# Attention scores of four heads: one kind to a stretch instead of half and half

## The chip, the core and the metric

The kernel runs on one core of a Trainium2 chip. The core has five engines, each with its own in-order queue: TensorE (PE, matmuls, with its weight loads shown apart as PEld), VectorE (DVE), ScalarE (ACT), GpSimd (POOL) and SyncE (SP, which issues the DMAs here). Matmuls write to PSUM, eight banks of 512 fp32 columns on 128 partitions; DVE and ACT read it. The metric is device time in microseconds of one execution, and a kernel's time is the median of its runs.

## The reference

For each of 16 sequences of 512 tokens with 512 channels, one transformer block: layer norm, attention of 32 heads of 16 channels, layer norm of its result and a residual sum; then layer norm, a gated feed-forward part of 1408 channels, layer norm, residual sum. The part the change touches is this:

```
q, k = rope(split_heads(x @ Wq.T + bq)), rope(split_heads(x @ Wk.T + bk))
scores = einsum('bhqd,bhkd->bhqk', q, k) / sqrt(dh)
scores = where(causal, scores, -inf)
weights = softmax(scores, axis=-1)
out = einsum('bhqk,bhkd->bhqd', weights, v)
```

The remaining lines are dense products: v, q, k and the output projection in fp32, gate, up and down products with split operands (a rounded part and the remainder) of type fp32r.

## The kernel before

**Groups and steps.** Four heads make a group, eight groups a batch (sequence), so there are 128 groups; group n is worked in five steps, `one_step(work, n, i)` for i = 0 to 4. A step emits, in this order: what earlier steps put off to it (`later`), in step 0 the loads of q and k of group n + 2 (`load_group`), one stretch of score matmuls (`scores`) with the ACT and DVE work on them, in step 2 the turning of the maxima (`turn_maxima`), a piece of dense work (`next(work)`), and in steps 3 and 0 the products of weights and values (`values`). All engines keep the order of the program: `InOrder` pins every instruction, so an instruction that waits holds back all that stand behind it on its engine.

**Two kinds of scores.** The softmax needs each row's maximum before the exponential. So the scores are computed twice. First as queries by keys (`S_PARTS`): DVE adds a mask of -1e30 on the diagonal blocks of 128 x 128 and takes the maximum along the keys, negated, into `nm`. `turn_maxima` transposes the 16 columns of maxima on PE (`pm`), ACT rounds them (`nmh`), DVE takes the remainder (`nml`), and a step later two DMAs place both as rows in `mx`. Then as keys by queries (`ST_PARTS`), with a third matmul that adds the negated maxima (`one` times `mx`): ACT takes the exponential of these straight into the weights `pa` and `pc`, POOL zeroes the part above the diagonal of diagonal blocks (`affine_select`), and `values` multiplies them with v. k is held as two fp32r pieces, `kh` and `kl`, so a part of the first kind takes two matmuls for each head, a part of the second kind three. The four heads sit in four strips of 32 rows, and their four matmuls run side by side; I call them a set.

**The banks.** Each head has one bank; `sc` is two tiles of two banks. In every step each bank holds both kinds, 256 columns each: the left half for weights, the right half for maxima (`at_s`). ACT and DVE work crosswise, ACT on the heads 0 and 1 while DVE has the heads 2 and 3, and then the other way round (lines 622 to 627). The next stretch begins when both are done, since its first set writes all four banks. A group's work on scores is 30 sets, ten exponentials of 512 elements, eight masks of 256, ten maxima of 512, and one small minimum that joins two partial maxima.

**The dense work.** `run_list` cuts the batch's list of dense products into pieces, one to a step, in proportion to `SHARES` (line 43), which gives a weight to each of the five steps; a unit of cost is four or two matmul passes of 512 columns, 0.27 for an fp32r matmul. It avoids a cut shortly after the end of a product. The products go through three PSUM buffers (`psum`, tag `d`), which a product's tail on ACT and DVE frees. Items such as `rest` and `store` of `qk_block` are laid behind a product at a given distance (`merge`). The tail and rest of a q or k block form a loop over ACT, DVE and POOL on single buffers `ya` and `ys`: ACT copies (`ys`), DVE multiplies with the cosine (`ya`), POOL multiplies with the sine, DVE adds, ACT rounds (`yh`), POOL subtracts (`yl`).

**Opening and end.** Before group 0 the maxima of groups 0 and 1 have to be made, in the steps from (-2, 2) on. The first list (v, q and k of the second batch) is spread over 46 of the 48 steps from there to the end of the first batch. The last batch has no q, k and v of a next one to make.

Of the kernel before, what the change touches and what calls it, by code (L numbers as in the profile page):

```python
# [24 lines left out]
NB = T // P  # L25
NC = C // P
NG = H // 4
WIDTH = H * W + 32 - W + 1
STEPS = 5
MM = 1.0  # L30
TR = 0.15
M1 = 0.27

HALF = T // 2
ST_PARTS = [[(0, 0, 256, 0)], [(0, 256, 256, 0)], [(1, 128, 256, 0)], [(1, 384, 128, 0), (3, 384, 128, 128)], [(2, 256, 256, 0)]]
S_PARTS = [[(3, 0, 256, 0)], [(3, 256, 256, 0)], [(0, 0, 128, 0), (2, 0, 128, 128)], [(2, 128, 256, 0)], [(1, 0, 256, 0)]]
S_DIAG = [None, 128, 0, 128, 128]  # L40
ST_DIAG = [0, None, 0, 128, 0]

SHARES = [2.3, 3.8, 3.8, 2.4, 3.5]


class InOrder:
# [14 lines left out]
class Block:  # L61
# [54 lines left out]
    def constants(self):  # L116
        nc, a, con = self.nc, self.a, self.const
# [23 lines left out]
        for name in ("bo", "dscale"):  # L141
# [3 lines left out]
        self.gh = con.tile([P, self.NF], FP, tag="gh", name="gh")  # L145
        self.gu = con.tile([P, self.NF], FP, tag="gu", name="gu")

        m = self.mask = con.tile([P, P], mybir.dt.bfloat16, tag="mask", name="mask")
        nc.gpsimd.memset(m, 0.0)
        nc.gpsimd.affine_select(  # L150
            out=m, in_=m, compare_op=ALU.is_ge, fill=-BIG, base=0, pattern=[[-1, P]], channel_multiplier=1
        )
        self.sc = [self.ps_sc.tile([P, 2, T], FP, tag=f"sc{k}", name="sc") for k in range(2)]
        self.v17 = []
        for i in range(2):
            t = con.tile([P, NB, WIDTH], FP, tag=f"v17_{i}", name=f"v17_{i}")
# [432 lines left out]
            ks.append(t)  # L589
        self.qs[n], self.ks[n] = q, ks  # L590

    def scores(self, n, m, i):

        todo = []
        st = 0 <= n < self.B * NG
        part = (i + 3) % STEPS
        at_s = HALF if n >= 0 or i % 2 else 0
        for j in range(4):
            r, r2 = slice(32 * j, 32 * j + 32), slice(32 * j, 32 * j + 2)
            todo.append([])  # L600
            if 0 <= m < self.B * NG:
                q, ks = self.qs[m], self.ks[m]
                for qb, k0, w, at in S_PARTS[part]:
                    at += at_s
                    out, x = self.sc[j // 2][:, j % 2, at : at + w], q[r, ts(qb, P)]
                    todo[-1] += [(out, x, ks[0][r, k0 : k0 + w], True, False), (out, x, ks[1][r, k0 : k0 + w], False, True)]
            if st:
                q, ks, mx = self.qs[n], self.ks[n], self.mxs[n]
                for kb, q0, w, at in ST_PARTS[i]:
                    out, x = self.sc[j // 2][:, j % 2, at : at + w], q[r, q0 : q0 + w]  # L610
                    todo[-1] += [
                        (out, ks[0][r, ts(kb, P)], x, True, False),
                        (out, ks[1][r, ts(kb, P)], x, False, False),
                        (out, self.one[r2, :], mx[r2, q0 : q0 + w], False, True),
                    ]

        for k in range(len(todo[0])):
            for t in todo:
                out, l, r, first, last = t[k]
                self.pe.matmul(out, l, r, start=first, stop=last)  # L620

        for two in (slice(0, 2), slice(2, 4)):
            other = slice(2 - two.start, 4 - two.start)
            if st:
                self.weights(n, i, two)
            if 0 <= m < self.B * NG:
                self.maxima(m, part, self.sc[other.start // 2][:, :, at_s : at_s + HALF], other)

    def maxima(self, m, part, s, two):
        if m not in self.nms:  # L630

            self.nms[m] = self.tile([P, 2, 4, NB], "nm", bufs=2)
        full = self.nms[m]
        nm = full[:, :, two]
        at = S_DIAG[part]
        if at is not None:
            d = s[:, :, at : at + P]
            self.dve.tensor_tensor(d, d, self.mask.unsqueeze(1).to_broadcast(list(d.shape)), ALU.add)
        out = [nm[:, 0, :, 3], nm[:, 1, :, 1], nm[:, :, :, 0].rearrange("p x j -> p j x"), nm[:, 0, :, 2], nm[:, 0, :, 1]][part]
        if part == 2:  # L640
            s = s.rearrange("p j (x t) -> p j x t", x=2)
        self.dve.tensor_reduce(out=out, in_=s, axis=AX.X, op=ALU.max, negate=True)
        if part == 4 and two.start == 0:
            self.dve.tensor_tensor(full[:, 0, :, 2:4], full[:, 0, :, 2:4], full[:, 1, :, 0:2], ALU.min)

    def turn_maxima(self, m):
        p = self.psum("pm")
        self.pe.transpose(p[0:16, 0:P], self.nms.pop(m)[:, 0].rearrange("p j b -> p (j b)"), self.ident)
# [11 lines left out]
    def weights(self, n, i, two):  # L660
        if i % 2 == 0 and two.start == 0:
            self.pts[n, i // 2] = self.tile([P, 4, HALF], "pc", bufs=1) if i == 4 else self.tile([P, 4, T], "pa", bufs=2)
        at = HALF * (i % 2)
        pt = self.pts[n, i // 2][:, :, at : at + HALF]
        self.act.activation(pt[:, two], self.sc[two.start // 2][:, :, 0:HALF], AF.Exp, scale=0.25)
        at = ST_DIAG[i]
        if at is not None and two.start:
            d = pt[:, :, at : at + P]
            self.pool.affine_select(
                out=d, in_=d, compare_op=ALU.is_ge, fill=0.0, base=0, pattern=[[0, 4], [1, P]], channel_multiplier=-1  # L670
            )

    def values(self, n, lot):
        b, g = divmod(n, NG)
        if lot == 0:
            self.avs[n] = self.ps_av.tile([P, T], FP, tag="av", name="av")
        av = self.avs[n]
        for kb, w, k, at in ([(0, 512, 0, 0)], [(1, 384, 1, 0), (3, 128, 1, 384), (2, 256, 2, 0)])[lot]:
            for j in range(4):
                h = 4 * g + j  # L680
                self.pe.matmul(
                    av[32 * j : 32 * j + 32, T - w : T],
                    self.v17[b % 2][:, kb, h * W : h * W + 32],
                    self.pts[n, k][:, j, at : at + w],
                    start=(kb == 0),
                    stop=(kb == 2),
                )
        if lot:
            for k in range(3):
                del self.pts[n, k]  # L690
# [27 lines left out]
    def run_list(self, L, steps, first=0):  # L718
# [109 lines left out]
    def one_step(self, work, n, i):  # L828
        for f, args in self.todo.pop(self.step, []):
            f(*args)  # L830
        if i == 0 and n + 2 < self.B * NG:
            self.load_group(n + 2)
        self.scores(n, n + 2 if i >= 2 else n + 1, i)
        if i == 2 and 0 <= n + 1 < self.B * NG:
            self.turn_maxima(n + 1)
        next(work, None)
        if i == 3 and 0 <= n < self.B * NG:
            self.values(n, 0)
        if i == 0 and 0 <= n - 1 < self.B * NG:
            self.values(n - 1, 1)  # L840
        self.step += 1

    def front(self):
# [152 lines left out]

    def batches(self):
        B = self.B
        work = self.run_list(self.first_list(), 46, 2)
        self.load_group(0)  # L1000
        for n, i0 in ((-2, 2), (-1, 0)):
            for i in range(i0, STEPS):
                self.one_step(work, n, i)
        for b in range(B):
            if b:
# [8 lines left out]
                work = self.run_list(L, NG * STEPS)  # L1014
# [4 lines left out]
        work = self.run_list(L + self.downs(B - 2, None, (0, 1), True, True), STEPS + 2)  # L1019
# [65 lines left out]
```

## Time and profile before

| what | value |
|---|---|
| median of 3 runs | 3304.48 us (3301.31 to 3305.98) |
| profiled execution | 3305.37 us |
| its span | 3303.5 us |
| mean granted PE clock | 0.974 of full speed |
| PE busy | 3036.6 us |
| DVE busy | 2168.4 us |
| ACT busy | 1602.6 us |
| POOL busy | 1326.7 us |
| DMA | 143 GB/s on the mean |

The profile is one execution. A line of the groups gives the engine, the operation, output and inputs by tile names, the shapes (partitions x elements) and the count; behind the first bar the busy time of the group and the mean of one in ns; behind the second the idle time of the engine just before them and what ended it. A line of the waits gives who waited for whom, the total, how often, and the longest. In the timeline the first number is the start, the second the duration, in us. Matmuls are pipelined, so their durations overlap: their cost is read from start to start.

### The profile page before, as it was taken

Reading aid. Unit: us, or ns where it says so; the run is one execution under the profiler, and the core shown is the slowest. Engines: PE = TensorE matmul, PEld = TensorE weight load, DVE = VectorE, ACT = ScalarE, POOL = GpSimd, SP = SyncE. Lnnn points to the kernel's source line nnn. Section 1 sums busy time; section 2 is a strip of 40 time slices with the busy share of each in tenths; the row PEclk is TensorE's granted clock in tenths of the full one; section 3 lists DMA queues with packets and bytes.
Section 4 is the critical chain, followed back from the end, with each engine's and each line's share of the span. In section 5 each row is a group of like instructions: output and inputs, shape, how many; then the busy total and the mean of one; then the engine's idle time right before and its main releaser. Section 6 shows DMA issues by size and latency. Waiting matters only on the chain. (4 is left out here: it accounts for less than half of the span.)

```text
span 3303.5 us, 69520 instructions
## 1 busy us (share of the span) xinstructions
PE 3036.6 (92%) x26378; PEld 1813.2 (55%) x26378; DVE 2168.4 (66%) x4253; ACT 1602.6 (49%) x2758; POOL 1326.7 (40%) x1677
## 2 busy tenths in 40 slices
PE   6778999999999999999999999999999999989898
PEld 3334564646556465554646556465564646546556
DVE  5565767766676676767767676676767766677743
ACT  5344545445544545545444554545445454554432
POOL 4133445343444424344342444424344442443443
PEclk9888999999999999999999999999999999999999
DMA  7444534535343453534445343453534445343322
GB/s 255 157 136 140 176 108 147 164 127 186 103 156 128 149 171 123 171 110 145 150 135 179 104 158 130 147 164 124 171 111 150 144 145 169 112 144 130 127 97 76
DMA packets 271973, 472.07 MB, mean 143 GB/s; under 512 B 45920, under 2 KB 50016, under 8 KB 271200
## 3 DMA queue, kind: packets, MB, share of 16 engines
q1 hardware_dynamic: 271200, 466.49, 43.4%
q8 instruction: 212, 3.47, 0.4%
q10 hardware_dynamic: 432, 1.05, 0.1%
q14 instruction: 129, 1.06, 0.1%
HBM read 345.79 MB, written 125.30 MB: 143 GB/s over the span
## 5 line engine op out<-in xcount | busy, mean ns | idle before, releaser
L56 ACT ACTIVATE pa<-sc 128x512 f32<-128x512 f32 x1024 | 607.0, 598 | 783.6 <-PE sc L56 409.0
L56 DVE TENSOR_REDUCE nm<-sc 128x2 f32<-128x512 f32 (+1 forms) x1280 | 877.0, 692 | 122.2 <-PE sc L56 86.5
L56 DVE TENSOR_TENSOR sc<-sc,mask 128x256 f32<-128x256 f32 x1024 | 437.2, 427 | 469.0 <-PE sc L56 396.8
L56 POOL TENSOR_SCALAR_AFFINE_SELECT pa<-pa 128x512 f32<-128x512 f32 x384 | 244.0, 636 | 969.7 <-ACT pa L56 631.9
L56 PEld LDWEIGHTS sc<-kh,q 32*128 32x128 f32 x3072 | 156.9, 186 | 492.9 <-issue 172.8
L56 PE MATMUL sc<-kh,q 32*128 32x256 f32 (+1 forms) x3072 | 276.9, 357 | 111.6 <-DVE nm L56 79.4
L56 PE MATMUL pd<-wd,hl 128*128 128x512 f32 x704 | 283.9, 403 | 24.7 <-POOL hl L56 24.7
L56 ACT ACTIVATE pc<-sc 128x512 f32<-128x512 f32 x256 | 151.4, 597 | 302.2 <-PE sc L56 175.3
L56 PE MATMUL pg<-xntf,wf 128*128 128x512 f32 x704 | 286.0, 406 | 9.7 <-DVE ya L56 6.4
L56 PE MATMUL pd<-wd,hh 128*128 128x512 f32 x704 | 289.0, 411 | 2.8 <-ACT hh L56 2.8
L56 POOL TENSOR_TENSOR hl<-ht,hh 128x512 fp32r<-128x512 f32 (+1 forms) x192 | 229.0, 1193 | 145.6 <-ACT hh L56 144.0
L56 PE MATMUL pg<-xntfl,wf 128*128 128x512 f32 x704 | 286.3, 407 | 0.2 <-DVE xntfl L56 0.2
L56 PE MATMUL av<-pa,v 128*32 128x512 f32 (+2 forms) x3072 | 282.4, 471 | 0.0
L56 PE MATMUL pu<-xntfl,wf 128*128 128x512 f32 x704 | 281.1, 399 | 0.0
L56 PE MATMUL pu<-xntf,wf 128*128 128x512 f32 x704 | 279.3, 397 | 0.0
L56 PE MATMUL pk<-xnta,w 128*128 128x512 f32 x480 | 259.4, 667 | 4.1 <-DVE ya L56 4.1
L56 POOL TENSOR_TENSOR yl<-ya,yh 128x512 fp32r<-128x512 f32 x128 | 162.9, 1273 | 201.9 <-ACT yh L56 201.9
L56 PE MATMUL pq<-xnta,w 128*128 128x512 f32 x480 | 236.9, 625 | 5.0 <-ACT xntf L56 4.3
L56 PE MATMUL po<-w,oc 128*128 128x512 f32 x512 | 238.4, 602 | 2.5 <-DMA w<-in_wo 2.0
L56 POOL TENSOR_TENSOR ln_rstd<-ln_ve,neghalf 128x1 f32<-128x1 f32 x256 | 146.8, 573 | 229.9 <-DVE ln_ve L56 229.7
L56 PE MATMUL sc<-q,kh 32*128 32x256 f32 (+1 forms) x3072 | 227.1, 279 | 0.1
L56 PE MATMUL sc<-mx,one 2*128 2x256 f32 (+1 forms) x3072 | 226.4, 277 | 0.1
(123 smaller groups left out, 5374.6 us busy)
## 6 DMA issues: line engine op xcount, KB each, us to landing
wf<-wgs SPq DMA_DIRECT2D x352, 256.0 KB
q<-qd SPq DMA_DIRECT2D x128, 256.0 KB
kh<-kd SPq DMA_DIRECT2D x128, 256.0 KB
kl<-kd SPq DMA_DIRECT2D x128, 256.0 KB
od<-ot SPq DMA_DIRECT2D x128, 256.0 KB
w<-in_wo SPq DMA_DIRECT2D x68, 256.0 KB
xr<-in_x SPq DMA_DIRECT2D x66, 256.0 KB
w<-in_wq SPq DMA_DIRECT2D x64, 256.0 KB
```

The costliest lines, as they stand in the source:

```text
L56: return self.tc.keep_in_program_order(f(*args, **kwargs))
```

## The change

A stretch now holds scores of one kind in steps 0 to 3, of up to 512 columns a head: in step 0 keys 0 to 127 by all 512 queries for weights; in step 1 the query blocks 2 (384 keys) and 0 (128 keys) for maxima; in step 2 the key blocks 3 (128 queries) and 1 (384 queries) for weights; in step 3 the query block 3 (512 keys) for maxima. Step 4 holds both, 256 columns each: key block 2 for weights, query block 1 for maxima. The maxima of step 1 are those of group n + 1, those of steps 3 and 4 of group n + 2 (`AHEAD`). `sc` is one tile of four banks. An exponential takes the four heads at once, 2048 elements in steps 0 and 2 and 1024 in step 4; so do mask and maximum. The mask tile is doubled to 256 columns for step 1, which has two diagonal blocks a head. POOL zeroes two blocks in one instruction in step 2. No maximum is in two parts any more, so the small minimum is gone. A group's work on scores is 20 sets, three exponentials, three masks, four maxima. The values follow in three bursts, at the end of steps 1, 3 and 0, instead of two. SHARES has new weights; the opening starts at step (-2, 3), and its list is spread over all of the 47 steps.

```diff
-ST_PARTS = [[(0, 0, 256, 0)], [(0, 256, 256, 0)], [(1, 128, 256, 0)], [(1, 384, 128, 0), (3, 384, 128, 128)], [(2, 256, 256, 0)]]
-S_PARTS = [[(3, 0, 256, 0)], [(3, 256, 256, 0)], [(0, 0, 128, 0), (2, 0, 128, 128)], [(2, 128, 256, 0)], [(1, 0, 256, 0)]]
-S_DIAG = [None, 128, 0, 128, 128]
-ST_DIAG = [0, None, 0, 128, 0]
-
-SHARES = [2.3, 3.8, 3.8, 2.4, 3.5]
+ST_SETS = [[(0, 0, 512, 0)], [], [(3, 384, 128, 0), (1, 128, 384, 128)], [], [(2, 256, 256, 0)]]
+S_SETS = [[], [(2, 384, 0), (0, 128, 384)], [], [(3, 512, 0)], [(1, 256, 256)]]
+AHEAD = [0, 1, 0, 2, 2]
+
+SHARES = [2.3, 3.1, 3.0, 2.8, 3.9]
...
-        self.sc = [self.ps_sc.tile([P, 2, T], FP, tag=f"sc{k}", name="sc") for k in range(2)]
+        self.sc = self.ps_sc.tile([P, 4, T], FP, tag="sc", name="sc")
...
-        for two in (slice(0, 2), slice(2, 4)):
-            other = slice(2 - two.start, 4 - two.start)
-            if st:
-                self.weights(n, i, two)
-            if 0 <= m < self.B * NG:
-                self.maxima(m, part, self.sc[other.start // 2][:, :, at_s : at_s + HALF], other)
+        if there(n) and ST_SETS[i]:
+            self.weights(n, i)
+        if there(m) and S_SETS[i]:
+            self.maxima(m, i)
+
+    def maxima(self, m, i):
+        if m not in self.nms:
+            self.nms[m] = self.tile([P, 4, NB], "nm", bufs=2)
+        w = P * len(S_SETS[i])
+        d = self.sc[:, :, T - w :]
+        self.dve.tensor_tensor(d, d, self.mask[:, 0:w].unsqueeze(1).to_broadcast(list(d.shape)), ALU.add)
+        for qb, w, at in S_SETS[i]:
+            self.dve.tensor_reduce(
+                out=self.nms[m][:, :, qb], in_=self.sc[:, :, at : at + w], axis=AX.X, op=ALU.max, negate=True
+            )
...
+    def weights(self, n, i):
+        w = HALF if i == 4 else T
+        pt = self.pts[n, i // 2] = self.tile([P, 4, w], "pc" if i == 4 else "pa", bufs=1 if i == 4 else 2)
+        self.act.activation(pt, self.sc[:, :, 0:w], AF.Exp, scale=0.25)
+        if i == 2:
+            d = pt[:, :, 0:HALF]
+            pat = [[0, 4], [0, 2], [1, P]]
+        else:
+            d, pat = pt[:, :, 0:P], [[0, 4], [1, P]]
+        self.pool.affine_select(out=d, in_=d, compare_op=ALU.is_ge, fill=0.0, base=0, pattern=pat, channel_multiplier=-1)
...
-        self.scores(n, n + 2 if i >= 2 else n + 1, i)
+        self.scores(n, i)
...
+        if i == 1 and 0 <= n < self.B * NG:
+            self.values(n, 0)
         if i == 3 and 0 <= n < self.B * NG:
-            self.values(n, 0)
+            self.values(n, 1)
         if i == 0 and 0 <= n - 1 < self.B * NG:
-            self.values(n - 1, 1)
+            self.values(n - 1, 2)
...
-        work = self.run_list(self.first_list(), 46, 2)
+        work = self.run_list(self.first_list(), 47, 3)
         self.load_group(0)
-        for n, i0 in ((-2, 2), (-1, 0)):
+        for n, i0 in ((-2, 3), (-1, 0)):
```

More of the change, by code (lines that the diff above doesn't have):

```diff
@@ L146, in constants @@
         self.gu = con.tile([P, self.NF], FP, tag="gu", name="gu")
-        m = self.mask = con.tile([P, P], mybir.dt.bfloat16, tag="mask", name="mask")
+        m = self.mask = con.tile([P, 2 * P], mybir.dt.bfloat16, tag="mask", name="mask")
         nc.gpsimd.memset(m, 0.0)
-        nc.gpsimd.affine_select(
-            out=m, in_=m, compare_op=ALU.is_ge, fill=-BIG, base=0, pattern=[[-1, P]], channel_multiplier=1
-        )
-        self.sc = [self.ps_sc.tile([P, 2, T], FP, tag=f"sc{k}", name="sc") for k in range(2)]
+        for i in range(2):
+            x = m[:, ts(i, P)]
+            nc.gpsimd.affine_select(
+                out=x, in_=x, compare_op=ALU.is_ge, fill=-BIG, base=0, pattern=[[-1, P]], channel_multiplier=1
+            )
+        self.sc = self.ps_sc.tile([P, 4, T], FP, tag="sc", name="sc")
         self.v17 = []
@@ L590, in load_group, with scores @@
         self.qs[n], self.ks[n] = q, ks
[L592 to L597, printed above, removed]
+    def scores(self, n, i):
+        m = n + AHEAD[i]
+        there = lambda g: 0 <= g < self.B * NG
+        todo = [[] for _ in range(4)]
         for j in range(4):
             r, r2 = slice(32 * j, 32 * j + 32), slice(32 * j, 32 * j + 2)
-            todo.append([])
-            if 0 <= m < self.B * NG:
[L602 to L606, printed above, removed]
-            if st:
[L608 to L611, printed above, removed]
+            if there(m):
+                for qb, w, at in S_SETS[i]:
+                    q, ks = self.qs[m], self.ks[m]
+                    out, x = self.sc[:, j, at : at + w], q[r, ts(qb, P)]
+                    todo[j] += [(out, x, ks[0][r, 0:w], True, False), (out, x, ks[1][r, 0:w], False, True)]
+            if there(n):
+                for kb, q0, w, at in ST_SETS[i]:
+                    q, ks, mx = self.qs[n], self.ks[n], self.mxs[n]
+                    out, x = self.sc[:, j, at : at + w], q[r, q0 : q0 + w]
+                    todo[j] += [
                         (out, ks[0][r, ts(kb, P)], x, True, False),
@@ L620, in scores @@
                 self.pe.matmul(out, l, r, start=first, stop=last)
-        for two in (slice(0, 2), slice(2, 4)):
-            other = slice(2 - two.start, 4 - two.start)
-            if st:
-                self.weights(n, i, two)
-            if 0 <= m < self.B * NG:
-                self.maxima(m, part, self.sc[other.start // 2][:, :, at_s : at_s + HALF], other)
-    def maxima(self, m, part, s, two):
-        if m not in self.nms:
[L632 to L644, printed above, removed]
+        if there(n) and ST_SETS[i]:
[3 more added lines that the diff above has]
+    def maxima(self, m, i):
+        if m not in self.nms:
+            self.nms[m] = self.tile([P, 4, NB], "nm", bufs=2)
+        w = P * len(S_SETS[i])
+        d = self.sc[:, :, T - w :]
+        self.dve.tensor_tensor(d, d, self.mask[:, 0:w].unsqueeze(1).to_broadcast(list(d.shape)), ALU.add)
+        for qb, w, at in S_SETS[i]:
+            self.dve.tensor_reduce(
+                out=self.nms[m][:, :, qb], in_=self.sc[:, :, at : at + w], axis=AX.X, op=ALU.max, negate=True
+            )
     def turn_maxima(self, m):
         p = self.psum("pm")
-        self.pe.transpose(p[0:16, 0:P], self.nms.pop(m)[:, 0].rearrange("p j b -> p (j b)"), self.ident)
+        self.pe.transpose(p[0:16, 0:P], self.nms.pop(m).rearrange("p j b -> p (j b)"), self.ident)
         hi, lo = [self.tile([16, P], i, bufs=1, dtype=FR) for i in ("nmh", "nml")]
@@ L658, in turn_maxima @@
         self.later(1, put)
[L660 to L671, printed above, removed]
+    def weights(self, n, i):
[8 more added lines that the diff above has]
+        self.pool.affine_select(out=d, in_=d, compare_op=ALU.is_ge, fill=0.0, base=0, pattern=pat, channel_multiplier=-1)
     def values(self, n, lot):
@@ L677, in values @@
         av = self.avs[n]
-        for kb, w, k, at in ([(0, 512, 0, 0)], [(1, 384, 1, 0), (3, 128, 1, 384), (2, 256, 2, 0)])[lot]:
+        pt = self.pts.pop((n, lot))
+        for kb, q0, w, at in ST_SETS[2 * lot]:
             for j in range(4):
@@ L683, in values @@
                     self.v17[b % 2][:, kb, h * W : h * W + 32],
-                    self.pts[n, k][:, j, at : at + w],
+                    pt[:, j, at : at + w],
                     start=(kb == 0),
@@ L687, in values @@
                 )
-        if lot:
-            for k in range(3):
-                del self.pts[n, k]
+        if lot == 2:
             del self.ks[n], self.qs[n], self.mxs[n]
```

## The prediction

> **What bounds the kernel now.** Read first the page's busy times, to see which engine leaves no room:
>
> ```profile
> PE 3036.6 (92%) x26378; PEld 1813.2 (55%) x26378; DVE 2168.4 (66%) x4253; ACT 1602.6 (49%) x2758; POOL 1326.7 (40%) x1677
> ```
>
> TensorE (PE) has work 92% of the span; VectorE (DVE) and ScalarE (ACT) do not fill theirs. So time comes from matmul time and from what makes PE wait. Next the groups by shape, for the price of each operation on scores:
>
> ```profile
> L56 DVE TENSOR_REDUCE nm<-sc 128x2 f32<-128x512 f32 x1024 | 699.6, 692 | 113.4 <-PE sc L56 86.5 <-ACT pa L56 0.3
> L56 ACT ACTIVATE pa<-sc 128x512 f32<-128x512 f32 x1024 | 607.0, 598 | 783.6 <-PE sc L56 409.0 <-DVE nm L56 347.0 <-PE pu L56 7.6
> L56 DVE TENSOR_TENSOR sc<-sc,mask 128x256 f32<-128x256 f32 x1024 | 437.2, 427 | 469.0 <-PE sc L56 396.8 <-ACT pa L56 56.1 <-ACT pc L56 11.1
> L56 PE MATMUL sc<-kh,q 32*128 32x256 f32 x2048 | 202.6, 383 | 69.5 <-DVE nm L56 37.3 <-ACT pa L56 7.8 <-ACT hh L56 7.0
> L56 PE MATMUL sc<-kh,q 32*128 32x128 f32 x1024 | 74.4, 305 | 42.2 <-DVE nm L56 42.1
> ```
>
> See that PE's waits ahead of a stretch of scores end with DVE's maxima. Then the waits, for what delays DVE itself:
>
> ```profile
> DVE ya L56 <- POOL yl L56: 122.9, 57, 2.2
> PE sc L56 <- DVE nm L56: 79.4, 82, 5.7
> PE pm L56 <- DVE ya L56: 37.0, 13, 3.0
> ```
>
> DVE stands still on `ya` (rotation of q and k) with the maxima queued behind it. Last the timeline of one step (a step 3 among gate and up products):
>
> ```profile
> 1597.85 0.39 PE L56 MATMUL sc<-kh,q 32*128 32x256 f32 x4
> ...
> 1598.70 0.28 PE L56 MATMUL sc<-mx,one 2*128 2x128 f32 x4
> 1598.91 0.50 PE L56 MATMUL pg<-xntfl,wf 128*128 128x512 f32 x1
> 1599.01 0.60 ACT L56 ACTIVATE pa<-sc 128x512 f32<-128x512 f32 x1 [2.82 <-PE sc L56]
> 1599.06 0.43 DVE L56 TENSOR_TENSOR sc<-sc,mask 128x256 f32<-128x256 f32 x1 [1.29 <-PE sc L56]
> ...
> 1600.31 0.60 ACT L56 ACTIVATE pa<-sc 128x512 f32<-128x512 f32 x1 [0.70 <-DVE nm L56]
> ...
> 1600.59 0.69 DVE L56 TENSOR_REDUCE nm<-sc 128x2 f32<-128x512 f32 x1
> ...
> 1600.95 1.07 PE L56 MATMUL av<-pa,v 128*32 128x512 f32 x8
> ...
> 1601.94 0.34 PE L56 MATMUL sc<-kh,q 32*128 32x128 f32 x4
> ```
>
> After the last set of four score matmuls (1598.70) ACT starts 0.31 us later, DVE 0.36; DVE ends at 1601.28, 2.22 us after its start. The next stretch writes the same four banks. Where PE stood waiting, it began about 0.15 us after the last reduce. Here it could have begun at 1601.43 and did at 1601.94: dense products and values filled the time, with 0.5 to spare. That **spare** is what the change alters.
>
> Means over groups 8 to 119, read start to start along the timeline: steps 0 to 4 last 4.83, 4.62, 5.34, 4.81, 4.88 us (24.48 a group). In them PE stands at the next stretch 0.17, 0.07, 0.00, 0.25, 0.06 (0.55; 62 us in all), and 0.34 at `pm` in step 2. Stretches take 0.80, 0.80, 0.83, 1.06, 1.04, values 1.43 (step 0) and 1.00 (step 3). Dense work is the rest, 24.48 - 0.89 - 4.53 - 2.43 = 16.63; a unit of SHARES is 16.63/15.8 = 1.053 us, and 16.63/15.1 = 1.101 after.
>
> **Part 1, score matmuls.** Start to start, a set of four takes 0.118 us at 256 columns, 0.111 at 128. Before: 20 x 0.118 + 10 x 0.111 = 3.47 us a group. After: five sets each of 512, 384, 256 and 128. No row has 512 or 384 in four strips; I take 0.229 (dense `pg`, same type, 512 columns) and halfway, 0.173: 5 x (0.229 + 0.173 + 0.118 + 0.111) = 3.16, **-0.31**. If 384 costs as 256 plus 128 and 512 as two 256s, nothing is gained; that is the dear end. The cheap end, half a 512 taken at 0.10, is -0.4.
>
> **Part 2, values.** Three bursts instead of two, same columns. 0.99 us for 512 columns and 1.43 for 768 give 0.0017 a column and 0.11 a burst: **+0.11**. Together -0.20 x 128 = **-25 us**.
>
> **Part 3, the consumers.** ACT: 512 elements cost 598 ns, and the casts of 512 and 1024 (617, 1042) give 0.83 ns an element: 2048 cost 1.87 us, 1024 1.02. DVE: 427 ns at 256 and 683 at 512 (`x<-po,bo`, `y<-pd,dscale`) give 1.0 an element: masks 0.69 (512) and 1.20 (1024), reduces 0.69, 1.20, 1.72, 2.23 for 512, 1024, 1536, 2048. A group's exponentials fall from 5.98 to 4.76 us, its masks and maxima from 10.5 to 8.4. None of that is on PE; it is worth only what it takes off waits.
>
> What PE sees is the chain of each step. Before, ACT and DVE worked side by side on two pairs of banks: offset of the last set + 0.36 + 2.22 + 0.15 = 3.31, 3.31, 2.39 (no mask), 3.58, 3.53. After, only one engine works in steps 0 to 3, and in step 4 DVE's mask waits for the exponential (same banks; the 347 us of `pa` waiting on `nm` show that a bank is not shared):
> step 0: 0.57 + 0.31 + 1.87 + 0.15 = 2.9; step 1: 0.57 + 0.36 + (1.20 + 1.72 + 0.69 + 0.08 of gaps) + 0.15 = 4.77; step 2: 0.79 + 0.31 + 1.87 + 0.15 = 3.12; step 3: 0.34 + 0.36 + 2.96 + 0.15 = 3.81; step 4: 0.58 + 0.31 + 1.02 + 0.05 + 1.93 + 0.15 = 4.04.
> Steps after, without waits (dense by SHARES, stretch, values): 2.53 + 0.90 + 0.55 = 3.98; 3.41 + 0.78 + 1.00 = 5.19; 3.30 + 1.09 = 4.39; 3.08 + 0.67 + 1.00 = 4.75; 4.29 + 0.80 = 5.09.
> **Spare before: 1.35, 1.24, 2.6, 0.98, 1.29. After: 1.1, 0.42, 1.27, 0.94, 1.05.** It shrinks from 7.5 to 4.8 us a group, most in step 1. Before, spares of 1.0 to 1.35 cost 0.06 to 0.25 in waits, as lengths scatter (0.3 to 0.7) and DVE starts late (in the latest tenth over 1.5 us after the last set). By that, steps 0, 3 and 4 cost 0.2 each, step 2 0.1, step 1 0.25: 0.95 against 0.55, **+0.4 x 112 = +45 us**. Cheap end -30: DVE, free in steps 0 and 2, starts on time and half the waits go. Dear end +90: step 1 waits 0.65 each time.
>
> [...]
>
> **Part 4, what else queues.** Rests of q and k (DVE add, ACT cast, POOL subtract) stand behind the score work of their step. It ends 3.2, 3.2, 2.5, 3.4, 3.4 us into the step now; after, 2.75 (ACT), 4.6, 3.6 (in step 2 `nml` waits for `nmh`, which stands behind the 1.87 us exponential and holds a PSUM buffer), 3.7, 3.9: half a microsecond later on the mean, in a loop whose next `ya` already waits for `yl`. Between -37 (the `pm` waits go) and +40 (they double); I take +5, near no change, since the list's cuts move too. POOL's select of 1024 elements replaces two of 512 (636 ns each); values come over a step later, so nothing. If that cover went, it would cost up to 0.6 a group. SP issues the same loads; a group's q and k are first needed in step 3 instead of 2, a step more of cover. The opening list is spread over 47 steps instead of 46 of 48; that shifts its loads by a fraction of a step, 0.
>
> **Part 5, where dense work is thin.** First batch (112 to 278 us): a step is its chain. Bare chains sum to 16.1 before (barest groups took 17.2, the mean 20.7) and 18.6 after: at most +20 us for 8 groups; at the least -10, as the prologue has a step less and a third of the excess over the bare chain may go. I take +8. Last batch (some 20 us a group): unit 0.87, step 1 lasts 4.49 against a chain of 4.77; 0.3 to 0.6 a group, +5.
>
> **Sum.** -25 + 45 + 5 + 8 + 5 = +38 on the profiled 3305.4 (span 3303.5): 3343. Its time is 0.9 over the median of 3304.48. I shade the waits to +40, since fewer of DVE's microseconds must help somewhat: 3337.
>
> **Rivals.**
> *Longer waits, as summed* (0.42): 3315 to 3365.
> *The backlog goes* (0.30), on the other side: DVE has no score work in steps 0 and 2, so step 1's mask starts 0.36 us after the last set, and the waits do not grow. For: 2.1 us a group less on DVE. Against: 0.42 spare in step 1. Waits unchanged, with parts 4 and 5 at zero: 3280; at the cheap end 3250. It decides where total waits rise by under 0.2 us a group.
> *About even* (0.10): waits rise by just that.
> *The q/k loop clogs* (0.12): later rests keep `ya` waiting and PE's three PSUM buffers full; `pm` waits double: 3337 + 35 = 3372, up to 3400.
> *The wider matmuls gain nothing* (0.06): +40: 3377.
>
> **Numbers.** Measurements of this kernel differ by some 0.2%, 6.6 us. Slower 0.42 + 0.12 + 0.06 = 0.60, same 0.10, faster 0.30. The range leaves out the cheapest tenth of the faster case and the dearest of the clogged one: 3265 to 3395. The likeliest case's own is 3315 to 3365.
>
> **What would show it.** Reduces of 2.2 us and exponentials of 1.87; score sets of 0.229 and 0.173; steps near 3.98, 5.19, 4.39, 4.75, 5.09 plus waits; PE's waits at the stretch after step 1 (ended by `nm`) the largest. Wrong: if those waits do not exceed today's 62 us, the kernel is faster; if `ya` on `yl` grows past 123 us, part 4 is too small.

## The result, and the profile after

The changed kernel takes 3318.52 us (median of 6 runs, 3313.78 to 3323.47) against 3305.23 for the kernel before in the same comparison (3298.50 to 3308.78): a ratio of 1.0042, with an interval of 1.0027 to 1.0057. It is slower, by 13.3 us and not by 32.5 as forecast. Its profiled execution has a span of 3318.4 us, 14.9 more than the one before; all sums below are made against these two spans.

The page of the changed kernel, busy times:

```profile
PE 3023.2 (91%) x21258; PEld 1679.7 (51%) x21258; DVE 1963.7 (59%) x2717; ACT 1478.7 (45%) x1862; POOL 1306.6 (39%) x1550
```

Every engine is busy for less time than before: DVE by 205 us, ACT by 124, PE by 13. The kernel got slower all the same, so PE stands still for longer. Next the groups by shape of the changed kernel, the operations on scores:

```profile
L54 ACT ACTIVATE pa<-sc 128x2048 f32<-128x2048 f32 x256 | 480.9, 1879 | 498.5 <-PE sc L54 482.9 <-DVE ln_mv L54 9.0 <-DVE sg L54 3.2
L54 DVE TENSOR_REDUCE nm<-sc 128x4 f32<-128x2048 f32 x128 | 293.5, 2293 | 4.4
L54 DVE TENSOR_REDUCE nm<-sc 128x4 f32<-128x1536 f32 x128 | 225.1, 1759 | 4.4
L54 DVE TENSOR_TENSOR sc<-sc,mask 128x512 f32<-128x512 f32 x256 | 177.7, 694 | 222.4 <-ACT pc L54 158.3 <-PE sc L54 64.0
L54 DVE TENSOR_TENSOR sc<-sc,mask 128x1024 f32<-128x1024 f32 x128 | 157.7, 1232 | 246.6 <-PE sc L54 226.1 <-ACT xn L54 13.7 <-ACT ot L54 5.2
```

The second number behind the first bar is the mean of one in ns: 1.88 us for an exponential of 2048, 2.29 and 1.76 for the wide maxima, 0.69 and 1.23 for the masks. ACT no longer waits for `nm` ahead of an exponential. And the waits, of PE and of what delays DVE (us in total, times, longest):

```profile
DVE nml L54 <- ACT nmh L54: 298.3, 128, 4.2
DVE ya L54 <- POOL yl L54: 176.7, 82, 2.2
DVE sc L54 <- ACT pc L54: 158.3, 112, 4.1
PE sc L54 <- DVE nm L54: 124.8, 125, 5.4
PE sc L54 <- ACT pa L54: 48.5, 51, 2.7
PE pm L54 <- DVE ya L54: 38.6, 13, 3.0
```

PE's waits ahead of the scores rose from 79.4 to 124.8 us (for `nm`) and from 7.8 to 48.5 (for `pa`). What fell is a wait that the prediction did not show. In the waits of the kernel before:

```profile
ACT pa L56 <- DVE nm L56: 347.0, 386, 2.3
ACT pc L56 <- DVE nm L56: 87.7, 109, 2.2
PEld px L56 <- ACT xn L56: 63.6, 44, 2.7
PE px L56 <- ACT xn L56: 37.7, 41, 1.8
```

In the changed kernel there is no wait of PE for `xn` from ACT, and of PEld 11.2 us are left.

Where the 14.9 us lie, read start to start along the timeline (a stretch is the run of score matmuls, values are the `av` matmuls; half-clock time is the time at a granted clock of 0.5, in which `pk` matmuls of 512 columns start 0.85 us apart instead of 0.43):

| us | before | after | difference |
|---|---|---|---|
| start to group 0 | 112.0 | 110.3 | -1.7 |
| groups 0 to 7 | 165.5 | 169.0 | +3.5 |
| groups 8 to 111 | 2562.9 | 2554.3 | -8.6 |
| — stretches and values, without waits | | | -23 |
| — PE's waits at the next stretch | 51.2 | 108.0 | +57 |
| — PE's waits between dense products, full clock | 73.8 | 23.4 | -50 |
| — into `pm`, from the matmul ahead of it | 59.4 | 67.3 | +8 |
| — half-clock time (costs about half of it) | 66.4 | 54.6 | -6 |
| groups 112 to 119 | 179.3 | 186.6 | +7.3 |
| groups 120 to 127 | 155.1 | 169.8 | +14.7 |

The five terms inside groups 8 to 111 come to -14; the 5 us to -8.6 are not placed. The row into `pm` holds the cost of the matmul ahead of it, 0.205 us before and 0.267 after, where the last set of the stretch is wider; the wait in it is 38.1 and 39.5 us, so 6 of the 8 us belong to the stretches. Over most of the run the changed kernel is thus no slower (8.6 us in one profiled execution of each is less than two executions of one kernel can differ: the runs of the kernel before lie up to 10.3 us apart), and the last sixteen groups, with little dense work to a step, lose 22 us: their waits at the stretch rise from 16.3 to 32.8 us, and their time at half clock from 17 to 41.

Two timelines show the two sides. Kernel before, dense work going on to a transposition of `xn`:

```profile
1720.62 0.42 DVE L56 TENSOR_TENSOR sc<-sc,mask 128x256 f32<-128x256 f32 x1
1720.80 0.60 ACT L56 ACTIVATE pa<-sc 128x512 f32<-128x512 f32 x1 [1.77 <-DVE nm L56]
1721.08 0.69 DVE L56 TENSOR_REDUCE nm<-sc 128x2 f32<-128x512 f32 x1
1721.29 0.80 ACT L56 ACTIVATE xn<-x,ln_sh,ln_rstd 128x512 f32<-128x512 f32 x1
...
1722.15 0.55 PE L56 MATMUL px<-ident,xn 128*128 128x128 f32 x3 [1.84 <-ACT xn L56]
```

The second exponential waits 1.77 us for the maxima of its banks; the normalisation `xn` stands behind it in ACT's queue; PE stands 1.84 us for `xn`. In the changed kernel the exponential has its stretch to itself and this wait is gone. The changed kernel, step 0 of a group among `pk` and gate products:

```profile
1562.59 0.41 PE L54 MATMUL sc<-mx,one 2*128 2x512 f32 x4
...
1565.72 0.62 ACT L54 CAST yh<-ya 128x512 fp32r<-128x512 f32 x1 [1.46 <-DVE ya L54]
1566.24 1.87 ACT L54 ACTIVATE pa<-sc 128x2048 f32<-128x2048 f32 x1
...
1568.17 0.45 PE L54 MATMUL sc<-kh,q 32*128 32x384 f32 x4 [1.29 <-ACT pa L54]
```

The last set of scores starts at 1562.59, the exponential 3.65 us later, because `yh` is ahead of it in the queue and waits for an answer from DVE. Then it takes 1.87 us in one piece, and PE stands for the rest. Of the 108 us of waits in groups 8 to 111, 92 lie in steps whose consumer began more than 0.8 us after the last set of scores.

That DVE's mask of step 4 waits 158.3 us for `pc`, the exponential of the other columns of the same banks, is an order like the one that the 347.0 and 87.7 us of ACT's waits showed in the old layout: at these banks the two engines work one after the other, on disjoint columns too. In the changed kernel none of the 384 exponentials overlaps in time with any of the 896 masks and maxima. The runs show the waits; what happens without this order no run shows, so the prediction's reading that a bank "is not shared" holds for the order of these programs.

### The profile page after: what moved, and what is told of

The parts are those of the page before. It is cut to its first block, busy times and chain, and to the rows that moved or that the text cites. A ratio compares the mean times of both kernels' runs of the same rounds, so it can differ in the third digit from the quotient of the medians.

```text
span 3318.4 us, 55663 instructions
## 1 busy us (share of the span) xinstructions
PE 3023.2 (91%) x21258; PEld 1679.7 (51%) x21258; DVE 1963.7 (59%) x2717; ACT 1478.7 (45%) x1862; POOL 1306.6 (39%) x1550
## 5 line engine op out<-in xcount | busy, mean ns | idle before, releaser
L54 DVE TENSOR_REDUCE nm<-sc 128x4 f32<-128x2048 f32 (+3 forms) x512 | 751.9, 1490 | 13.2
L54 ACT ACTIVATE pa<-sc 128x2048 f32<-128x2048 f32 x256 | 480.9, 1879 | 498.5 <-PE sc L54 482.9
L54 DVE TENSOR_TENSOR sc<-sc,mask 128x512 f32<-128x512 f32 (+1 forms) x384 | 335.4, 873 | 469.0 <-PE sc L54 290.1
L54 POOL TENSOR_SCALAR_AFFINE_SELECT pa<-pa 128x512 f32<-128x512 f32 (+1 forms) x256 | 223.0, 871 | 808.9 <-ACT pa L54 808.9
L54 PE MATMUL sc<-kh,q 32*128 32x512 f32 (+3 forms) x2048 | 205.7, 391 | 108.7 <-DVE nm L54 57.9
L54 PE MATMUL pg<-xntf,wf 128*128 128x512 f32 x704 | 290.1, 412 | 12.2 <-DVE ya L54 10.3
L54 ACT ACTIVATE pc<-sc 128x1024 f32<-128x1024 f32 x128 | 131.3, 1026 | 311.6 <-PE sc L54 257.4
L54 PEld LDWEIGHTS sc<-kh,q 32*128 32x128 f32 x2048 | 100.4, 186 | 324.2 <-DVE nm L54 130.8
L54 PE MATMUL sc<-q,kh 32*128 32x512 f32 (+3 forms) x2048 | 196.1, 372 | 69.4 <-DVE nm L54 66.8
L54 POOL TENSOR_SCALAR_AFFINE_SELECT pc<-pc 128x512 f32<-128x512 f32 x128 | 81.6, 637 | 412.9 <-ACT pc L54 412.8
```

The source lines that it names most:

```text
L54: return self.tc.keep_in_program_order(f(*args, **kwargs))
```

## The experiments

Theories: **A**, the old order held ACT behind the maxima, and with it normalisations and dense work; taking that away is what the change gains. **B**, the waits between dense products hang on where the list is cut. **S**, the waits at the stretches come from steps too short for their chain, so the shares set them. **Late start**, they come from consumers that begin late behind queued work.

### 1. The old shares

```diff
-SHARES = [2.3, 3.1, 3.0, 2.8, 3.9]
+SHARES = [2.3, 3.8, 3.8, 2.4, 3.5]
```

> The changed kernel with the old SHARES (2.3, 3.8, 3.8, 2.4, 3.5): dense work moves from steps 3 and 4 to steps 1 and 2. Theory S (PE's waits at a stretch follow the spare time of the step before, step length less chain): spare of steps 0 to 4 becomes 0.98, 1.0, 1.97, 0.39, 0.45 us instead of 1.1, 0.42, 1.27, 0.94, 1.05, so over groups 8 to 111 the mean wait after step 1 falls from 0.25 to about 0.1 us, after step 3 it rises from 0.38 to 0.8 and after step 4 from 0.08 to 0.4; waits there go from 108 to about 170 us, the time to 3360 to 3390. Rival D (the waits come from DVE being late on q/k work, not from step lengths): waits change by under 20 us. On the dense waits that the change took away (from the last output projection to the transposes, from down products to the transposes, 43 us in all): theory A (the exponential no longer waits for the maxima, so the cast and scale work behind it on ACT is on time) says they stay away; rival B (the list is merely cut elsewhere by the new SHARES) says that some 40 us of them come back.

Measured: 3407.14 us, ratio 1.0319 [1.0296, 1.0343]. Waits at the stretch: step 1 from 0.25 us a group to 0, step 3 from 0.38 to 0.66, step 4 from 0.08 to 0.22. The wait for `xn` behind an output block (`po` to `px`, 25.9 us before) did not come back, as A says. The one behind a down block (`pd` to `px`, 16.6 before, none in the changed kernel) did, with 34.2 us: that one hangs on where the list is cut, not on ACT's waits for maxima. It is still ACT's queue, with other work ahead of `xn`:

```profile
1088.53 0.62 ACT L54 CAST hh<-ht 128x512 fp32r<-128x512 f32 x1 [3.14 <-PE pd L54]
1089.05 1.87 ACT L54 ACTIVATE pa<-sc 128x2048 f32<-128x2048 f32 x1
1090.97 0.81 ACT L54 ACTIVATE y<-y,ln_sh,ln_rstd 128x512 f32<-128x512 f32 x1
1091.68 0.80 ACT L54 ACTIVATE xn<-x,ln_sh,ln_rstd 128x512 f32<-128x512 f32 x1
1092.54 0.69 PE L54 MATMUL px<-ident,xn 128*128 128x128 f32 x2 [2.46 <-ACT xn L54]
```

Half-clock time in groups 8 to 111 rose from 55 to 140 us. The time lies above S's 3360 to 3390. With the old shares the layout alone makes the kernel 3.2% slower, and the new shares win some 90 us of that back. What new shares would give the old order was not measured, so how much of the change's result is owed to the layout and how much to newly fitted shares stays open.

### 2. Shares moved to the steps that wait

```diff
-SHARES = [2.3, 3.1, 3.0, 2.8, 3.9]
+SHARES = [2.3, 3.6, 2.2, 3.3, 3.7]
```

> The changed kernel with SHARES 2.3, 3.6, 2.2, 3.3, 3.7: dense work moves from step 2, after which PE never waits, to steps 1 and 3. Theory S: spare 1.1, 0.97, 0.39, 1.5, 0.83 us, so the waits after steps 1 and 3 (0.25 and 0.38 us) fall to about 0.1 and 0.15, and 0.2 to 0.4 appear after step 2; the sum over groups 8 to 111 goes from 108 to 70 to 100 us, the time from 3318 to 3290 to 3315; in the last 16 groups the waits after step 1 (0.7 to 1.1 us) halve. Rival D: waits after steps 1 and 3 stay within 0.05 us.

Measured: 3302.97 us, ratio 1.0007 [0.9993, 1.0021]. Step 1's wait went (0.25 to 0.02), step 3's stayed (0.38 to 0.36) though the step had more work, and step 2 began to wait (0 to 0.38). In groups 8 to 111 the waits even rose, from 108.0 to 115.6 us, where S had said 70 to 100; that these groups still took 11 us less is not explained by these waits. The last sixteen groups fell from 356 to 344. The time lies in S's range, but S holds for step 1 only and fails for step 3, where DVE starts late.

### 3. The old order, with both exponentials first

```diff
-        for two in (slice(0, 2), slice(2, 4)):
-            other = slice(2 - two.start, 4 - two.start)
+        both = slice(0, 2), slice(2, 4)
+        for two in both:
             if st:
                 self.weights(n, i, two)
+        for two in both[::-1] if part == 4 else both:
             if 0 <= m < self.B * NG:
-                self.maxima(m, part, self.sc[other.start // 2][:, :, at_s : at_s + HALF], other)
+                self.maxima(m, part, self.sc[two.start // 2][:, :, at_s : at_s + HALF], two)
```

> The kernel before with its crosswise order undone: in every step ACT takes both exponentials first and DVE follows pair by pair, so that no exponential waits for a maximum (before: 435 us of such waits on ACT). Theory A: the dense waits at the transposes (27 us behind the output projection, 17 us behind the down products, groups 8 to 111) go, as they did with the change. Rival B: they stay. Theory S: the chain of steps 0, 1, 3 and 4 is 0.5 to 0.7 us longer (DVE starts behind the first exponential), spare falls to some 0.4 to 0.8, and the waits at the stretches rise from 51 to about 95 us; time within 15 us of before by A and S together, 3340 to 3350 by S and B.

Measured: 3454.01 us, ratio 1.0472 [1.0445, 1.0498]. Its waits:

```profile
DVE sc L56 <- ACT pa L56: 521.0, 266, 5.7
PE sc L56 <- DVE nm L56: 116.3, 173, 5.2
PE sc L56 <- issue: 52.6, 43, 2.4
PE px L56 <- ACT xn L56: 19.2, 14, 1.7
```

ACT no longer waits for DVE, and the `po` to `px` wait fell from 25.9 to 0, as A says; the 19.2 left are the `pd` to `px` ones. But the wait was handed to DVE (521 us), which frees the banks one pair late: the stretches of steps 0, 1 and 4 lengthen from 0.80, 0.80 and 1.04 to 1.07, 1.10 and 1.33 us, PE standing between the two pairs, and half-clock time rises from 66 to 147 us. The time is more than 100 us above both forecasts; neither had a price for the wait between the two pairs. With both kinds in a bank one of the two engines paid in both orders: ACT 435 us, or DVE 521.

### 4. The new order without mask additions

```diff
-        w = P * len(S_SETS[i])
-        d = self.sc[:, :, T - w :]
-        self.dve.tensor_tensor(d, d, self.mask[:, 0:w].unsqueeze(1).to_broadcast(list(d.shape)), ALU.add)
```

> The changed kernel without the mask additions on DVE: the maximum is taken over the whole diagonal block, keys after the query included, which is an upper bound of the row's maximum and only shifts the exponent, so the softmax is the same. The chains of steps 1, 3 and 4 shorten by 1.24, 0.73 and 0.73 us. Theory S: their spare becomes about 1.7, 1.7 and 1.8 us, the waits at the stretches over groups 8 to 111 fall from 108 to some 40 us and in the last 16 groups from 33 to under 10; time about 3318 - 68 - 25 = 3225 to 3250. Rival D: only the share of the waits in which DVE starts on time goes, a third or less, 3280 to 3300.

The maxima are then taken over whole diagonal blocks, masked keys too; the weights are still masked by POOL, so the softmax is the same as long as no masked score exceeds the row's own maximum so far that the exponentials vanish. Measured: 3153.61 us (3151.48 to 3160.96), ratio 0.9552 [0.9534, 0.9571], more than either theory gave. Its busy times and PE's waits:

```profile
PE 2972.6 (94%) x21258; PEld 1664.6 (53%) x21258; DVE 1629.2 (52%) x2333; ACT 1480.1 (47%) x1862; POOL 1308.9 (41%) x1550
```

```profile
PE sc L54 <- ACT pa L54: 50.6, 43, 2.8
PE sc L54 <- DVE nm L54: 48.4, 52, 5.6
PE pm L54 <- DVE ya L54: 22.2, 13, 1.8
```

In groups 8 to 111 108 us went: 55 of waits at the stretches (DVE's 124.8 became 48.4, ACT's 48.5 stayed), 18 of waits between dense products, 17 into `pm`, and half-clock time fell from 55 to 7, worth some 24. The last sixteen groups took 26 us less, the first eight 18, the start 7. A mask on 1024 elements costs 1.23 us of DVE, which for PE is nothing by itself; what it costs is the end of the chain in steps 1, 3 and 4 and the start of everything behind it in DVE's queue.

### 5. The old order without mask additions

```diff
-        at = S_DIAG[part]
-        if at is not None:
-            d = s[:, :, at : at + P]
-            self.dve.tensor_tensor(d, d, self.mask.unsqueeze(1).to_broadcast(list(d.shape)), ALU.add)
```

> The earlier order of the scores with its mask additions left out (the maxima are taken over the whole diagonal block; the softmax is the same). Theory A (in the earlier order ACT stood in its queue behind a bank's maxima; the masks made these long, and ACT's waits on them held up normalisations and with them TensorE's dense work): ACT's 435 us of waits on the maxima fall below 200, TensorE's dense waits from 96 to 40-60 us, the stretch waits from 51 to about 30, half-clock time by some 60 us: 3190-3225 us, so the new order without masks (3153.6) is faster than it by 1% or more. Rival (the masks cost both orders alike, so the change stays within a per cent of the old order whatever the masks do): 3140 us, 13 below the new order without masks.

Measured: 3185.09 us, ratio 0.9632 [0.9611, 0.9652]. Of its waits:

```profile
ACT pa L56 <- DVE nm L56: 147.3, 364, 1.9
ACT pc L56 <- DVE nm L56: 37.3, 93, 2.5
PE sc L56 <- DVE nm L56: 34.6, 44, 5.1
PE px L56 <- ACT xn L56: 10.5, 28, 1.1
```

As A says, ACT's 435 us for `nm` fell to 185 and the dense waits from 73.8 to 33.1. The waits at the stretches fell to 10.7, more than expected, half-clock time by 21 us and not 60, and the time lies 5 us under the range. The two kernels without masks stand at 0.9552 and 0.9632 of the kernel before, intervals apart: without masks the change is a gain of 0.8%, a little under the 1% expected, and groups 8 to 111 go from 2480.5 to 2446.2. That is within the per cent that the rival allowed, but its premise fails: the masks cost the new order 4.9% of its time and the old one 3.7%. So the sign of the change hangs on how long DVE's part of a step is. The old layout lets ACT and DVE work side by side and hides the masks at the cost of ACT's queue; the new one puts them in one row.

### 6. The turned maxima ahead of the scores

```diff
-        self.scores(n, i)
         if i == 2 and 0 <= n + 1 < self.B * NG:
             self.turn_maxima(n + 1)
+        self.scores(n, i)
```

> The changed kernel with the turning of the next group's maxima put ahead of the scores of a group's third step and not behind its 2048-element exponential. Late-start theory (most of the waits at the stretches come from consumers that start late, because DVE stands 2.3 us a group in the subtraction that waits for ScalarE's copy of the turned maxima behind that exponential): VectorE's 298 us of waits there fall below 60, the stretch waits after the third and fourth steps fall by a third or more (0.38 to 0.25 us a group), 3285-3305 us. Rival (that wait lies in VectorE's idle time and nobody waits for what is behind it): the same 298 us go, the time stays at 3311-3325 us; if the transposition, now at the head of the step, waits for a PSUM buffer, it holds the scores and the time is up to 20 us longer.

Measured: 3342.18 us, ratio 1.0112 [1.0095, 1.0129]: 24 us worse than without the move.

```profile
PE sc L54 <- DVE nm L54: 59.6, 82, 3.9
PE pm L54 <- DVE ya L54: 52.5, 13, 4.1
PE pm L54 <- DVE nm L54: 46.8, 44, 2.9
DVE nml L54 <- ACT nmh L54: 30.8, 53, 1.5
```

DVE's 298 us became 31 and step 3's wait fell from 0.38 to 0.19 us a group, as the late-start theory says. But the transposition itself needs the maxima of step 1, and at the head of the step PE now waits for them (46.8 us) without the scores to fill the time. Into `pm` go 138.4 us in place of 67.3; without the matmul ahead, now a values matmul of 0.52 us, the wait rises from 39.5 to 84.0. Half-clock time in groups 8 to 111 rises from 55 to 92. The expectation had a price at this place, up to 20 us, but for a PSUM buffer. The place behind the scores costs DVE idle time and saves PE's.

> The same move of the turned maxima in the changed kernel with its mask additions left out (3153.6 us without the move). Late-start theory: 3130-3146 us, the wait after the fourth step from 0.19 to below 0.1 us a group. Rival: 3149-3158 us.

Measured: 3194.06 us, ratio 0.9665 [0.9649, 0.9682], 40 worse than without the move. Step 3's wait went (0.19 to 0), the stretch waits fell from 52.7 to 32.5 us, the waits at `pm` rose from 22.9 to 36.9 (50.7 to 91.3 with the matmul ahead), and half-clock time from 7 to 85. Neither expectation had that price.

### 7. Other shares without masks

> The changed kernel without mask additions, with the shares of the dense work 2.7, 3.1, 2.6, 3.0, 3.7 in place of 2.3, 3.1, 3.0, 2.8, 3.9: about 0.4 us of work more in the first step and 0.2 in the fourth, where its waits are (0.31 and 0.19 us a group), taken from the third and fifth, which wait for nothing. Theory that a share sets the wait: these two fall to 0.1 and 0.1, 35 us in all with nothing given back: 3115-3135 us. Rival (the waits are late starts and move with the dense work): 3148-3162 us, with waits in the third or fifth step instead.

Measured: 3200.95 us, ratio 0.9682 [0.9664, 0.9700], 47 worse and above both ranges. Step 0's wait did not move (0.31) though the step had more work; step 3's went (0.19 to 0.01); step 2 began to wait (0 to 0.20, all but 2 us of it where the exponential stands behind a cast `hh` in group 7); the waits between dense products at full clock came back (5.8 to 19.2 us), and half-clock time (7 to 48). Step 0's wait lies in the same 26 steps as without the new shares, groups 0 and 4 of each batch, where ACT starts late behind `y` (11.6 us) and `yh` (20.6 us). There a larger share did not help a consumer that had not begun.

### 8. Two pieces of ScalarE work issued later

In `dense`, for a batch's last k block, and in `downs`:

```diff
-            self.merge(L, rest, 3)
-            self.merge(L, store, 5.5)
+            last = name == "k" and c == NC - 1
+            self.merge(L, rest, 5 if last else 3)
+            self.merge(L, store, 7.5 if last else 5.5)
...
-            self.merge(L, rest, 4)
-            self.merge(L, store, 8)
+            self.merge(L, rest, 5.5)
+            self.merge(L, store, 9)
```

> The changed kernel with two pieces of queued work issued later: the rounding of a batch's last k block (ScalarE's yh) after five units of dense work instead of three, and the scaling of a down block (ScalarE's y) after 5.5 instead of four. Nothing is computed differently. Late-start theory (in groups 0 and 4 of a batch the first step's exponential starts 2.6 to 3.6 us after its scores because it stands in ScalarE's queue behind yh or y, which wait for VectorE's and GpSimd's answers; the waits that follow are 20.4 and 10.3 us of the 108): the wait after the first step falls from 0.32 to below 0.12 us a group, nothing comes back elsewhere, and with a few spells at half clock less the time is 3280-3300 us. Chain-length theory (the 2048-element exponential itself is too long for the first step): the wait after the first step stays at 0.25 or more, 3312-3325 us.

Measured: 3298.68 us, ratio 1.0000 [0.9984, 1.0017]. Of the 21.3 us between the two profiled spans 17.7 lie in groups 8 to 111.

```profile
PE sc L54 <- DVE nm L54: 125.4, 133, 5.4
PE sc L54 <- ACT pa L54: 33.9, 40, 2.8
```

Nothing is computed in another way and no step is longer, and the loss is gone. Step 0's wait fell from 0.32 to 0.17 us a group, not below 0.12: behind `yh` the wait vanished (the exponential of the step shown above now starts 1.8 us after the last set instead of 3.6, and PE does not wait for it), while in group 0 of each batch one `y` still stands ahead of an exponential (11.8 us).

> The same two delays in the changed kernel without mask additions (3153.6 us; 32 of its 53 us of waits stand behind yh and y). Late-start theory: 3115-3135 us. Chain-length theory: 3148-3160 us.

Measured: 3152.82 us, ratio 0.9557 [0.9530, 0.9584]: no gain over 3153.61, and in the range of the chain-length theory. The waits fell as the late-start theory says, from 52.7 to 27.2 us, but half-clock time in groups 8 to 111 rose from 7 to 38, so a wait less was not a microsecond less.

### 9. Both rearrangements that helped

Experiments 2 and 8 together.

> The changed kernel with both rearrangements that took time off it apart: the shares of the dense work 2.3, 3.6, 2.2, 3.3, 3.7 (3302.97 by themselves, 15.5 below it) and the two later pieces of ScalarE work (19.8 below it by themselves), masks kept. If the two act on different waits (the shares on those after the second step and in the last batches, the later pieces on those after the first step) the gains add: 3278-3290 us, below the kernel before. If both only shift late starts about, or meet in the same spells at half clock: 3295-3305 us.

Measured: 3292.00 us, ratio 0.9972 [0.9960, 0.9984]. With its masks kept the new order is then 0.3% faster than the kernel before. The time lies between the two ranges. Against the kernel before, each in its own comparison, the changed kernel's ratio of 1.0042 falls by 0.35% with the shares, by 0.42% with the later pieces and by 0.70% with both: within the intervals the two gains add up. (The 15.5 and 19.8 us of the expectation set medians of different comparisons against each other.) Fastest of all is the version without mask additions, 3152.8 to 3153.6.

## Why the prediction was right in sign and wrong in size

**Part 1** held: sets of 512, 384, 256 and 128 columns took 0.229, 0.177, 0.118 and 0.111 us; 0.173 had been taken for 384. **Part 2** held: values cost 0.13 a group more, 0.11 forecast.

**Part 3**, the durations, held within 0.06 us each (1.88, 1.03; 0.69, 1.23; 0.68, 1.23, 1.76, 2.29). The waits at the stretches rose by 57 us in groups 8 to 111 and 7.7 in the next eight, against +45 for the 112: some 20 us too small. But step 1 is not the largest (step 0 to 4: 0.32, 0.25, 0.00, 0.38, 0.08). Spare time in a step was the wrong measure for step 0: experiment 7 gave it more and left 0.31 as it was; experiment 8 changed only what stands ahead in ACT's queue and halved its wait. For step 3 it was right in part: with masks more work left 0.36 (experiment 2) and less work brought 0.66 (experiment 1), and without masks more work took its wait from 0.19 to 0.01 (experiment 7). The hope behind the cheap end, that DVE "starts on time" once it is free in steps 0 and 2, failed: it is not free there, it stands behind `nml` and `ya`.

**The step that failed is part 4, "what else queues", taken at +5.** It followed the rests of q and k and the `pm` waits (38.1 us, then 39.5), and never priced ACT's 435 us of waits for `nm`, though the row of the exponentials showed 347.0 of them. The sentence in part 3 that less work on ACT is "worth only what it takes off waits" was right, and the wait that it took off was not looked up: normalisations stand behind those exponentials, and PE's dense work behind the normalisations. That is -50 us in groups 8 to 111, of which experiment 3 ties two parts to ACT's waits for the maxima: `po` to `px` (25.9 us) and `pd` to `pd` (17.5 before, 5.7 in the changed kernel, 1.9 with the exponentials first). The first is the surer: in experiment 5, where ACT's waits more than halve, `po` to `px` falls to some 5 us but `pd` to `pd` only to 14.6. The 16.6 of `pd` to `px` are owed at least in part to where the list is cut: they come back with the old shares and stay with the exponentials first (experiments 1 and 3), though without masks they halve. Against these stand 3.9 us more between `pu` and `pg`.

That the sign came out right is partly luck. For the groups up to 119 the forecast was a loss; measured, groups 8 to 119 are 1.3 us faster and the first eight 3.5 slower, and the loss of the whole is that of the last eight groups, for which 5 us had been set.

**Part 5** was too small at the end and too large at the start: +14.7 for the last batch against +5, +1.8 for start and first batch together against +8. In the last batch step 1 waits 1.07 us a group where 0.3 to 0.6 had been summed for the whole group, step 3 waits 0.58, and 17 us more run at half clock, which costs about half of that. Experiments 2 and 4 confirm the cause, too little dense work over a DVE chain that takes 4.08 us from the last set of step 1 to the next stretch at the least: more of it, or a shorter chain, takes 12 and 26 us off the last sixteen groups.

In groups 8 to 111 the larger matmuls, less the third burst of values, are worth some 17 us (the 23 of the table less the 6 ahead of `pm`), and the waits at the stretches grow by 57. Of the rivals, "the backlog goes" named the right side of the ledger but the wrong engine: ACT's queue cleared, not DVE's. "The q/k loop clogs" is answered by `ya` on `yl`: 176.7 us against 122.9, yet the `pm` waits hardly moved.

## What to carry to other kernels

When an in-order engine shows a large wait, ask what stands behind the waiting instruction and who waits for that: the price of a wait can be paid in another line of the profile (here behind ACT's 435 us of waits for `nm` stood PE's 25.9 us from `po` to `px`). A consumer that starts late may not be helped by more time in its step (step 0 here was not); look at what is queued ahead of it, and move that. And before two engines' work is separated by stages, look at what their overlap was hiding: here masks of 2.6 us a group (two of 0.69, one of 1.23) turned a gain of 0.8% into a loss of 0.4%.

## What the runs showed of the hardware

PE's granted clock fell to 0.50 not only after pauses of 2.3 to 3.0 us ahead of `pm` but also after some of 1.50 to 1.84 us. Three windows of 3.4 us of the kernel before (columns: window, length, busy time and count of PE, PEld, DVE, ACT and POOL, granted clock, DMA share, GB/s):

```profile
1521.60:1525.00 3.40, 1.57 (x6) 0.50 (x5) 3.14 (x8) 1.63 (x4) 2.53 (x4) 1.00 0.00 1
1525.00:1528.40 3.40, 3.40 (x35) 1.57 (x37) 2.53 (x8) 0.45 (x1) 1.75 (x6) 0.55 0.50 130
1528.40:1531.80 3.40, 3.40 (x20) 1.81 (x17) 2.50 (x5) 2.04 (x4) 1.83 (x2) 0.95 0.82 239
```

In the first PE stood 1.83 us for `xn` and was busy for 1.57; the next 3.4 us run at 0.55 of the clock, though PE is then busy throughout. In groups 8 to 111 spells at 0.50 last 3.41 or 6.83 us; there are 15 before, 12 in the changed kernel and 2 without masks, and they follow windows in which PE was busy for 14 to 59% of the time. In these groups of the first two kernels every window of 3.41 us (of the grid on which the spells begin) with PE busy for less than 40% was followed by one, 18 in all, but only 9 of 28 with 41 to 59% (windows outside a spell): pauses of 1.82 us were followed by a spell in some places and not in others, and why stays open. In a spell `pk` matmuls of 512 columns start 0.853 us apart, outside one 0.429 (medians of both kernels). By these a spell costs half its length, as an estimate: 1.7 us for one of 3.41 and 3.4 for one of 6.83. Where PE is otherwise busy, a wait of 1.5 to 1.8 us in the wrong place can thus cost that much more, and small waits have prices that jump: experiments 7 and 8 show 31 to 41 us of half-clock time more with no such difference in the waits.
